# Scatters ahead of a turn's layernorm steps, angle table by chunk with clearing on another engine, last roots by ScalarE

## The chip, the cores and the metric

The kernel runs on one core of a Trainium2 chip. Times are device microseconds (us) of that core; the time of a version is the median of its runs. The engines named below are TensorE (PE; its weight loads are shown as PEld), VectorE (DVE), ScalarE (ACT), GpSimd (POOL) and SyncE (SP). SP only issues DMAs here. Each engine works through its own instructions in the order in which they were put on its queue, and waits on semaphores for what the others produce.

## The reference

Sixteen sequences of 512 tokens with 128 channels pass through a linear attention block and a mixture of experts, each followed by a layernorm over the sum with its input. What matters, shortened:

```python
q, k, v = silu(x @ Wq), silu(x @ Wk), x @ Wv      # 16 heads of 8
lrpe(t) = concat(t * cos(theta * pos), t * sin(theta * pos))
energy = einsum('bhnd,bhmd->bhnm', lrpe(q), lrpe(k)) * tril
out = layernorm((energy @ v) @ Wo * sigmoid(x @ G1 @ G2)) * gamma + beta
x = layernorm(x + out)
probs = softmax(rmsnorm(x) @ router.T)            # 8 experts, 2 a token, capacity 1280
routed = scatter_add(expert(x[dispatch]) * weight)
shared = (silu(x @ sg) * (x @ su)) @ sd
x = layernorm(x + shared + routed)
```

## The kernel before

The tokens are cut into 64 tiles of 128, four to a sequence. The work has four stages.

**Opening.** Constants are made: masks, cleared buffers and the table `cst_tok` of cosines and sines, four chunks of 128 positions, which every sequence shares. `theta` is loaded with one DMA that writes the same row to all 128 partitions (L201). VectorE multiplies it by the positions (L318, L319), brings the angles into range (L320 to L325; chunk 0 first, then chunks 1 to 3 in one go), and ScalarE takes the sines (L330). GpSimd meanwhile writes the masks and clears, one after the other, four pairs of value buffers (`vpad`, `vlow`, L291 and L294), `zero` (L301) and `empty` (L303). The product G1 G2 is put into the weight tile `W` by VectorE (L335); the first projection waits for it.

**Attention turns.** A loop over turns t from -2 to 64 works on three tiles at a time, and its program order is the order on every engine. A turn projects tile t+2 (`project`: pq on PE; six ScalarE instructions; `hat` by VectorE L386), transposes tile t+1 (`turn_over`: pt on PE; kT, q, qT by ScalarE), makes the energies of tile t (`energies`: 32 small matmuls L444, masked to `et` by VectorE L451), and the values of tile t-1 (`values`: up to 56 small matmuls L468, L477, L486; `oT` by ScalarE L492), and then the state of tile t+1 (`remember`, L422, L433). Between them, `advance(turns)` gives the generator `after(b)` of a finished sequence one step (output projection, two layernorms, transposing for the router): its roots are taken by GpSimd with a power of -0.5 (L109), as is `rms` (L542). `sprinkle` gives the router one or more steps, and `shared(t)` puts in a step of the shared expert. At the end of a turn, `scatter_behind` issues two scatters: each is an indirect DMA by GpSimd (L671) that writes 128 rows of x1 to their experts' slots in DRAM. The first is put behind a one-column product `beat` (L688) that waits for `oT` of tile t-1. The DRAM buffers are cleared by 16 DMAs of SyncE, one in each of turns 0 to 15 (`fill`), eight from `zero`, eight from `empty`.

**Experts.** Eight experts, 1280 rows each; the results are scattered back by GpSimd.

**End.** The rest of the shared expert's steps runs on PE; beside it, `add_up` adds the experts' rows and `finish_lot` normalises a lot of tiles: statistics on VectorE (L101, L103), variance plus epsilon (L107), the root by GpSimd (L109), minus mean times root (`nb`, L910), then one ScalarE instruction for each tile (`res`, L913), and a DMA out. The last sequence is four lots of one tile. Each call of `an_end` advances one lot by one step; once the shared steps are used up, lots follow one another.

The turn of the loop, at its end (lines of the profile):

```python
            if 0 <= t + 1 < NT:
                remember(t + 1)
            advance(turns, "narrow")
            advance(turns)
            sprinkle(t, 4)
            if left:

                scatter_behind(oTs[(t - 1) // NC][:, ds((t - 1) % NC * P, 1)])
                scatter_behind()
```

Of the kernel before, what the change touches and what calls it, by code (L numbers as in the profile page):

```python
# [10 lines left out]
F32 = mybir.dt.float32  # L11
I32 = mybir.dt.int32
AF = mybir.ActivationFunctionType
ALU = mybir.AluOpType
# [5 lines left out]
P = 128  # L20
# [15 lines left out]
C1 = 6.28125  # L36
C2 = 2029.0 / 2 ** 20
C3 = 2.0 * math.pi - C1 - C2
# [9 lines left out]
def tile_kernel(  # L48
# [37 lines left out]
    nc.gpsimd.memset(neghalf, -0.5)  # L86
    x1 = keep.tile([P, NT, R], F32, name="x1")
# [23 lines left out]


    def shared_steps(b):
# [6 lines left out]
        def gate_half(i):  # L120
            if i % half == 0:
                h[i // half] = hp.tile([P, half, N], F32, tag="h", name=f"h_{b}_{i}")
            pool, tag = home["g"]
            pg = pool.tile([P, N], F32, tag=tag, name=f"pg_{b}_{i}")
            nc.tensor.matmul(pg, sg_sb[:, ts(i, P)], seq, start=True, stop=True)  # L125
            sl = sp.tile([P, N], F32, tag="sl", name=f"sl_{b}_{i}")
            nc.scalar.activation(sl, pg, AF.Silu)  # L127
            h["s", i] = sl

# [30 lines left out]
    done = set()  # L160
    latest = [None]
# [15 lines left out]
    with ExitStack() as ph:  # L177
# [21 lines left out]
        with tc.manual_schedule(engines=ORDERED):  # L199
            th_sb = cst.tile([P, D + HALF], F32, name="th_sb")  # L200
            nc.sync.dma_start(th_sb, theta.partition_broadcast(P))  # L201
# [15 lines left out]
            nc.gpsimd.memset(rw_sb, 0.0)  # L217
# [3 lines left out]
            load_x(1)  # L221
# [3 lines left out]
            nc.sync.dma_start(bet, beta.partition_broadcast(P))  # L225

# [19 lines left out]
            expi = cst.tile([P, E], I32, name="expi")  # L246
            nc.gpsimd.iota(expi, pattern=[[1, E]], base=0, channel_multiplier=0)
            expf = cst.tile([P, E], F32, name="expf")
            nc.vector.tensor_copy(expf, expi)
            first = cst.tile([P, E], F32, name="first")  # L250
            nc.vector.tensor_scalar(first, expf, -1.0, float(E), ALU.mult, ALU.add)
            startrow = cst.tile([P, E], F32, name="startrow")
            nc.vector.tensor_scalar(startrow, expf, float(CAP), float(-NSLOT), ALU.mult, ALU.add)
            count = cst.tile([P, E], F32, name="count")
            nc.vector.memset(count, 0.0)
            goes_on = {}
            for n in sorted({(b1 - b0) * NC for b0, b1 in groups}):
                goes_on[n] = cst.tile([P, E, n + 1], F32, name=f"goes_on{n}")
                nc.gpsimd.memset(goes_on[n], 1.0)
                nc.gpsimd.memset(goes_on[n][:, :, 0], 0.0)  # L260


            ones = cst.tile([P, P], F32, name="ones")
            nc.vector.memset(ones, 1.0)

            causal = cst.tile([P, 3, HALF], F32, name="causal")
            nc.gpsimd.memset(causal, 1.0)
            for block, at in ((0, 0), (0, HALF), (1, HALF), (2, 0)):
                rows = causal[at : at + HALF, block, :]
                nc.gpsimd.affine_select(  # L270
                    rows, rows, pattern=[[1, HALF]], compare_op=ALU.is_ge, fill=0.0, base=0, channel_multiplier=-1
                )
            tri = cst.tile([P, P], F32, name="tri")
            nc.gpsimd.affine_select(
                tri, ones, pattern=[[1, P]], compare_op=ALU.is_gt, fill=0.0, base=0, channel_multiplier=-1
            )
# [7 lines left out]
            )  # L284


            NVP = 4
            vpads = []
            for i in range(NVP):
                vp = cst.tile([P, 4, 4, 40], F32, name=f"vpad{i}")  # L290
                nc.gpsimd.memset(vp, 0.0)  # L291

                vl = cst.tile([P, 8, 40], F32, name=f"vlow{i}")
                nc.gpsimd.memset(vl, 0.0)  # L294
                vpads.append((vp, vl))
# [4 lines left out]
            zero = hp.tile([P, 4 * N], F32, tag="h", name="zero")  # L300
            nc.gpsimd.memset(zero, 0.0)  # L301
            empty = hp.tile([P, NS, R], F32, tag="h", name="empty")
            nc.gpsimd.memset(empty, 0.0)  # L303
            nc.gpsimd.memset(empty[:, :, D], NOBODY)


            pg = ps_w.tile([P, D], F32, tag="w", name="pg12")
            nc.tensor.matmul(pg, g1t_sb, g2_sb, start=True, stop=True)

            cst_tok = cst.tile([P, NC, 2, 16, 2, 8], F32, name="cst_tok")
            scratch = hp.tile([P, 2, NC, D + HALF], F32, tag="h", name="scratch")
            ang, turns_ = scratch[:, 0], scratch[:, 1]
            for c0, c1 in ((0, 1), (1, NC)):
                a, k = ang[:, c0:c1, :], turns_[:, c0:c1, :]
                for c in range(c0, c1):
                    nc.vector.tensor_scalar(ang[:, c, 0:D], th_sb[:, 0:D], pos[:, 0, c : c + 1], None, ALU.mult)  # L318
                    nc.vector.tensor_scalar(ang[:, c, D:], th_sb[:, D:], pos[:, 1, c : c + 1], None, ALU.mult)  # L319
                nc.vector.tensor_scalar(k, a, 1.0 / (2.0 * math.pi), MAGIC, ALU.mult, ALU.add)  # L320
                nc.vector.tensor_scalar(k, k, MAGIC, None, ALU.subtract)
# [5 lines left out]
                for c in range(c0, c1):  # L327
                    for s, (from_, scale, bias) in enumerate([(turns_, -1.0, half_pi), (ang, 1.0, 0.0)]):
                        for to, n0, n1 in ((cst_tok[:, c, 0], 0, D), (cst_tok[:, c, 1, 1::2], D, D + HALF)):
                            nc.scalar.activation(  # L330
                                to[:, :, s, :], from_[:, c, n0:n1].rearrange("p (h d) -> p h d", d=8), AF.Sin,
                                scale=scale, bias=bias,
                            )
                if c0 == 0:
                    nc.vector.tensor_copy(  # L335
                        W[:, 0:384].rearrange("p (h n) -> p h n", n=24)[:, :, 8:16], pg.rearrange("p (h d) -> p h d", d=8)
                    )
            for c0, c1 in ((0, 1), (1, NC)):
                nc.vector.tensor_copy(
                    cst_tok[:, c0:c1, 1, 0::2].rearrange("p c h s d -> p c h (s d)"),  # L340
                    cst_tok[:, c0:c1, 0, 0::2].rearrange("p c h s d -> p c h (s d)"),
                )
            nc.vector.tensor_scalar(wo_sb, wo_sb, 0.5, None, ALU.mult)
            nc.vector.tensor_copy(x1[:, :, D], toki)
# [14 lines left out]
        def project(t):  # L359
# [376 lines left out]
        with tc.manual_schedule(engines=ORDERED):  # L736
            for t in range(-2, NT + 1):
                coming, here, left = 0 <= t + 2 < NT, 0 <= t < NT, 0 <= t - 1 < NT
                stopped("wait")
                if coming:  # L740
                    if (t + 2) % NC == 0 and 2 <= (t + 2) // NC + 1 < B:
                        load_xT((t + 2) // NC + 1)
                        load_x((t + 2) // NC + 1)
                    project(t + 2)
                if t == 2:
# [54 lines left out]
    with ExitStack() as ph:  # L800
# [96 lines left out]
        def finish_lot(lot):  # L897
# [8 lines left out]
            rs = rstd_of(mv[:, :, 1], n, LN_EPS)  # L906
            yield True
            yield True
# [120 lines left out]
```

## Time and profile before

| what | value |
|---|---|
| time, median of 3 runs (lowest, highest) | 888.75 us (888.18, 888.76) |
| the profiled execution's own time | 912.27 us |
| its span, from the first to the last instruction | 910.6 us |
| mean granted TensorE clock | 0.981 |
| busy share of the span: PE, DVE, ACT, POOL | 93%, 61%, 49%, 38% |
| DMA share, 0 to 25, 25 to 50, 50 to 75 us | 0.88, 1.00, 0.22 |
| first matmul that works on tokens (pq, L363) | 14.22 us |
| last matmul ends | 888.81 us |
| last `res` of ScalarE starts | 901.64 us |

The views used are the page (busy time, the span in slices, the chain of work that ended last, groups of instructions), the chain and the timeline for chosen stretches, and the waits. In the chain each line is a start, a duration and what was waited for or done; "issue" is time in which an engine waited for nothing that the profile shows. In the timeline a line is start, duration, engine, line of the kernel, operation, output <- inputs, with the idle time before it in brackets and what ended it.

The profiled execution took 23.5 us longer than the median of the plain runs, so places in it and sums over it are its own.

### The profile page before, as it was taken

The page shows a single profiled execution, that of the slowest core. Times are in us where ns is not written, and L with a number is a line of the kernel's source. Part 1 is how long each engine was busy: PE and PEld are TensorE (multiplying, and loading weights), DVE is VectorE, ACT ScalarE, POOL GpSimd, SP SyncE. Part 2 cuts the span into 40 slices and gives each one's busy share as a digit, 9 for nine tenths or more (in the row PEclk, how much of TensorE's full clock was granted, in tenths as well). Part 3 has the DMA queues.
Part 4 walks back from the last instruction along what each step waited for, and adds up shares of the span by engine and source line. Part 5 has one row for each costly group of instructions (what it writes and reads, how often), then busy time and mean ns, then how long its engine had stood idle before and what let it go on. Part 6 is the DMA issues. An engine that isn't in the chain of part 4 may idle for free.

```text
span 910.6 us, 24496 instructions
## 1 busy us (share of the span) xinstructions
PE 843.0 (93%) x9790; PEld 576.5 (63%) x9790; DVE 557.1 (61%) x1687; ACT 442.3 (49%) x1285; POOL 344.2 (38%) x455
## 2 busy tenths in 40 slices
PE   2898999999998999989999999999999999999990
PEld 1676667666755776674566657776677766666670
DVE  6588788987688788878743333333333325884542
ACT  3677677566576757745522223333333332334332
POOL 4023222155655645566666703333333331010011
PEclk9999999999999999999999999999999999999996
DMA  8941111011111111000000053222231004641001
GB/s 288 417 146 33 31 32 32 24 34 55 44 50 50 55 32 39 26 22 22 12 8 2 2 159 94 77 68 60 84 91 62 27 24 125 177 135 34 25 24 46
DMA packets 64338, 62.97 MB, mean 69 GB/s; under 512 B 6179, under 2 KB 55130, under 8 KB 63200
## 3 DMA queue, kind: packets, MB, share of 16 engines
q1 hardware_dynamic: 57392, 50.44, 17.5%
q0 software_dynamic: 6656, 10.69, 3.7%
q8 instruction: 77, 1.26, 0.6%
q14 instruction: 37, 0.30, 0.1%
q10 hardware_dynamic: 176, 0.27, 0.1%
HBM read 32.71 MB, written 31.88 MB: 71 GB/s over the span
## 4 chain that ended last, share of the span: by engine, by line
PE 78%; DVE 14%; issue 3%; ACT 3%; DMA 1%; POOL 0%; POOLq 0%; DVEq 0%; ACTq 0%
PE pd L143 11%; PE pg L125 11%; PE pu L133 11%; PE ped L856 8%; PE peg L940 8%; PE peu L942 8%; PE pe L444 4%; PE pq L363 4%; DVE et L451 4%; PE pout L486 3%; PE pt L399 2%; PE pout L477 2%; PE pout L468 1%; PE po L501 1%; DVE st L101 1%
## 5 line engine op out<-in xcount | busy, mean ns | idle before, releaser
L109 POOL TENSOR_TENSOR rstd<-ve,neghalf 128x4 f32<-128x4 f32 (+1 forms) x51 | 52.4, 1028 | 259.0 <-DVE ve L107 224.0
L671 POOL DMA_INDIRECT xg_dram<-x,idx x128 | 132.2, 1033 | 37.7 <-issue 32.1
L127 ACT ACTIVATE sl<-pg 128x512 f32<-128x512 f32 x128 | 76.0, 596 | 127.6 <-PE pg L125 113.2
L862 POOL DMA_INDIRECT y_dram<-y,to x80 | 77.6, 970 | 154.2 <-ACT y L860 154.2
L945 DVE TENSOR_TENSOR eh<-esl,peu 128x512 f32<-128x512 f32 (+1 forms) x96 | 57.5, 599 | 128.1 <-PE peu L942 123.7
L125 PE MATMUL pg<-x1T,sg_sb 128*128 128x512 f32 x256 | 134.0, 605 | 2.1 <-DVE h L134 0.9
L451 DVE TENSOR_TENSOR et<-pe,causal 128x384 f32<-128x384 f32 x256 | 124.4, 547 | 18.0 <-PE pe L444 17.8
L134 DVE TENSOR_TENSOR h<-sl,pu 128x512 f32<-128x512 f32 x128 | 87.6, 684 | 75.5 <-PE pu L133 57.6
L133 PE MATMUL pu<-x1T,su_sb 128*128 128x512 f32 x256 | 131.4, 595 | 0.4 <-DVE x1T L148 0.4
L143 PEld LDWEIGHTS pd<-sd_sb,h 128*128 128x128 f32 x1024 | 119.6, 193 | 5.5 <-issue 5.5
L143 PE MATMUL pd<-sd_sb,h 128*128 128x128 f32 x1024 | 122.6, 276 | 0.0
L856 PEld LDWEIGHTS ped<-rd,eh 128*128 128x128 f32 x640 | 84.0, 192 | 24.6 <-issue 22.7
L940 PE MATMUL peg<-xgT,rg 128*128 128x512 f32 (+1 forms) x192 | 84.6, 522 | 0.0
L942 PE MATMUL peu<-xgT,ru 128*128 128x512 f32 (+1 forms) x192 | 84.4, 521 | 0.0
L856 PE MATMUL ped<-rd,eh 128*128 128x128 f32 x640 | 84.3, 275 | 0.0
L944 ACT ACTIVATE esl<-peg 128x512 f32<-128x512 f32 (+1 forms) x96 | 50.5, 526 | 56.0 <-PE peg L940 53.9
L133 PEld LDWEIGHTS pu<-x1T,su_sb 128*128 128x128 f32 x256 | 46.1, 192 | 45.8 <-issue 39.3
L860 ACT ACTIVATE y<-ped,wt 128x128 f32<-128x128 f32 x80 | 29.4, 367 | 84.6 <-PE ped L856 79.9
L125 PEld LDWEIGHTS pg<-x1T,sg_sb 128*128 128x128 f32 x256 | 44.8, 193 | 39.0 <-issue 33.9
L363 PE MATMUL pq<-W,xT 128*128 128x384 f32 x128 | 61.5, 564 | 7.8 <-DVE W L335 6.9
L444 PE MATMUL pe<-q,kT 32*64 32x192 f32 x2048 | 61.9, 338 | 0.8 <-issue 0.8
L386 DVE TENSOR_TENSOR hat<-qk,cst_tok 128x512 f32<-128x512 f32 x64 | 45.5, 711 | 23.3 <-ACT qk L371 22.6
(164 smaller groups left out, 1285.6 us busy)
## 6 DMA issues: line engine op xcount, KB each, us to landing
y_dram<-zero SPq DMA_DIRECT2D x8, 1024.0 KB
y<-y_dram SPq DMA_DIRECT2D x32, 256.0 KB, 3.2
xT<-xt SPq DMA_DIRECT2D x16, 384.0 KB, 6.5
xg_dram<-empty SPq DMA_DIRECT2D x8, 660.0 KB, 15.7
xg<-xg_dram SPq DMA_DIRECT2D x8, 660.0 KB
x<-x SPq DMA_DIRECT2D x16, 256.0 KB, 4.6
o<-res SPq DMA_DIRECT2D x15, 256.0 KB, 2.3
xg_dram<-x,idx POOLq DMA_INDIRECT x128
```

Source lines behind the costliest of these rows:

```text
L125: nc.tensor.matmul(pg, sg_sb[:, ts(i, P)], seq, start=True, stop=True)
L133: nc.tensor.matmul(pu, su_sb[:, ts(i, P)], seq, start=True, stop=True)
L134: nc.vector.tensor_tensor(h[i // half][:, i % half, :], h.pop(("s", i)), pu, ALU.mult)
L143: nc.tensor.matmul(pd, h[k][:, i - k * half, ts(c, P)], sd_sb[:, i, :], start=(i == 0), stop=(i == IS // P - 1))
L363: nc.tensor.matmul(pq[:, :, 0:24], xts[b][:, c, 0:P], W[:, 0:384].rearrange("p (h n) -> p h n", n=24), start=True, stop=True)
L444: nc.tensor.matmul(pes[g][mine, s], kT[rows, s, mine], q2[rows, s, 3 * i : 3 * i + 3], start=(s == 0), stop=(s == 1),)
L451: nc.vector.tensor_tensor(et.rearrange("p s k n -> p s (k n)"), pes[g].rearrange("p s k n -> p s (k n)"), causal.rearrange("p k n -> p (k ...
L671: i = nc.gpsimd.indirect_dma_start(out=xg_dram[:, :], out_offset=bass.IndirectOffsetOnAxis(ap=idx[:, k, t : t + 1], axis=0), in_=x1[:, t, ...
L856: nc.tensor.matmul(pd, h[:, i, ts(c, P)], got[e][2][:, i, :], start=(i == 0), stop=(i == IR // P - 1))
L862: i = nc.gpsimd.indirect_dma_start(out=y_dram[:, :], out_offset=bass.IndirectOffsetOnAxis(ap=to[:, at : at + 1], axis=0), in_=y, in_offset ...
L940: nc.tensor.matmul(pg[:, :n], rg_sb[:, ts(i, P)], xgTs[e][:, ds(o0, n)], start=True, stop=True)
L942: nc.tensor.matmul(pu[:, :n], ru_sb[:, ts(i, P)], xgTs[e][:, ds(o0, n)], start=True, stop=True)
```

## The change

Four things are edited.

*Opening.* `theta` is loaded as one row to one partition and spread to all by a matmul with ones (`pth`), copied to `th_sb` by ScalarE; the loads of g1t, g2 move from ScalarE's queue to SyncE's, and the first tile's quarter of xT is loaded ahead of the rest. VectorE makes the angles one chunk at a time (`angles`), with a reduction in two parts instead of three; chunks 0 and 1 before the loop, 2 and 3 in turns 0 and 1 (`beginning`), with the sines of 1, 2, 3 in turns -1, 0, 1. GpSimd clears only two of the four pairs of value buffers, and a product with an angle of chunk 0 holds it until those angles are done; the other two pairs, `zero` and `empty` are cleared by ScalarE copies of a zero column (`nought`), the last two at the end of turns 0 and 1. The copy of G1 G2 into `W` goes from VectorE to ScalarE. On ScalarE's queue the sines of chunk 0 stand behind the six instructions of the first projection. Constants of the router are made at the end of turn 2.

*Fills.* The 16 clearing DMAs start one turn later.

*Turn.* The two scatters stand ahead of the turn's second pair of `advance` calls. On GpSimd's queue this moves the second root of each sequence (L109) and `rms` (L542) behind the two scatters of their turn; the first root of a sequence, which is issued in the middle of a turn, stays ahead. No other engine's order changes by it.

*End.* Behind the last Silu, ScalarE loads its table for Sqrt, and lots that take their root after that take it on ScalarE, with a reciprocal on VectorE (`rstd_by_root`), in place of L107 and L109: three lots of four tiles and the four of one. One waiting step less is taken for them.

```diff
+    def rstd_by_root(var, n):
+
+        root = small.tile([P, n], F32, tag="ve", name="root")
+        nc.scalar.activation(root, var, AF.Sqrt, bias=eps_col)
+        r = small.tile([P, n], F32, tag="rstd", name="rstd")
+        nc.vector.reciprocal(r, root)
         return r
...
+            if (b, i) == (B - 1, IS // P - 1):
+
+                warm_root = small.tile([P, 1], F32, tag="warm_root", name="warm_root")
+                nc.scalar.activation(warm_root, eps_col, AF.Sqrt)
+                roots.append(warm_root)
...
-            th_sb = cst.tile([P, D + HALF], F32, name="th_sb")
-            nc.sync.dma_start(th_sb, theta.partition_broadcast(P))
+            th_row = cst.tile([1, D + HALF], F32, name="th_row")
+            nc.sync.dma_start(th_row, theta.unsqueeze(0))
...
-            load_xT(0)
             g1t_sb = cst.tile([8, D], F32, name="g1t_sb")
-            nc.scalar.dma_start(g1t_sb, g1t)
+            nc.sync.dma_start(g1t_sb, g1t)
             g2_sb = cst.tile([8, D], F32, name="g2_sb")
-            nc.scalar.dma_start(g2_sb, g2)
+            nc.sync.dma_start(g2_sb, g2)
+            xts[0] = wk2.tile([P, NC, P + HALF], F32, tag="xT", name="xT_0")
+            nc.sync.dma_start(xts[0][:, 0:1], xt[0, :, 0:1])
+            nc.sync.dma_start(xts[0][:, 1:], xt[0, :, 1:])
+            ones = cst.tile([P, P], F32, name="ones")
+            nc.vector.memset(ones, 1.0)
+            zcol = cst.tile([P, 1], F32, name="zcol")
+            nc.vector.memset(zcol, 0.0)
...
+                if i < 2:
+                    nc.gpsimd.memset(vp, 0.0)
+                    nc.gpsimd.memset(vl, 0.0)
+            def nought(tile_, n):
+                nc.scalar.copy(tile_, zcol.to_broadcast([P, n]))
+            pth = ps_w.tile([P, D + HALF], F32, tag="w", name="pth")
+            nc.tensor.matmul(pth, ones[0:1, :], th_row, start=True, stop=True)
+            th_sb = cst.tile([P, D + HALF], F32, name="th_sb")
+            nc.scalar.copy(th_sb, pth)
+            pg = ps_w.tile([P, D], F32, tag="w", name="pg12")
+            nc.tensor.matmul(pg, g1t_sb, g2_sb, start=True, stop=True)
+            for vp, vl in vpads[2:]:
+                nought(vp.rearrange("p a b d -> p (a b d)"), 640)
+                nought(vl.rearrange("p a d -> p (a d)"), 320)
+            nc.scalar.copy(
+                W[:, 0:384].rearrange("p (h n) -> p h n", n=24)[:, :, 8:16], pg.rearrange("p (h d) -> p h d", d=8)
+            )
...
+            turns_of = cst.tile([P, D + HALF], F32, name="turns_of")
+            nc.vector.tensor_scalar(turns_of, pth, 1.0 / (2.0 * math.pi), None, ALU.mult)
+        def angles(c, th):
+            a, size, k, whole = scratch[:, c], scratch[:, NC + c], scratch[:, 8], scratch[:, 9]
+            both = ((slice(0, D), pos[:, 0, c : c + 1]), (slice(D, D + HALF), pos[:, 1, c : c + 1]))
+            for m, at in both:
+                nc.vector.tensor_scalar(k[:, m], turns_of[:, m], at, MAGIC, ALU.mult, ALU.add)
+            nc.vector.tensor_scalar(whole, k, MAGIC, -C1, ALU.subtract, ALU.mult)
+            for m, at in both:
+                nc.vector.scalar_tensor_tensor(a[:, m], th[:, m], at, whole[:, m], ALU.mult, ALU.add)
+            nc.vector.tensor_scalar(k, k, MAGIC, -C2, ALU.subtract, ALU.mult)
+            nc.vector.tensor_tensor(a, a, k, ALU.add)
+            nc.vector.scalar_tensor_tensor(size, a, -1.0, a, ALU.mult, ALU.max)
+            nc.vector.tensor_scalar(a, a, -PI_BELOW, PI_BELOW, ALU.max, ALU.min)
+        def sines(c):
+            for s, (from_, scale, bias) in enumerate([(scratch[:, NC + c], -1.0, half_pi), (scratch[:, c], 1.0, 0.0)]):
+                for to, n0, n1 in ((cst_tok[:, c, 0], 0, D), (cst_tok[:, c, 1, 1::2], D, D + HALF)):
+                    nc.scalar.activation(
+                        to[:, :, s, :], from_[:, n0:n1].rearrange("p (h d) -> p h d", d=8), AF.Sin,
+                        scale=scale, bias=bias,
+                    )
+        def same(c):
+            nc.vector.tensor_copy(
+                cst_tok[:, c, 1, 0::2].rearrange("p h s d -> p h (s d)"),
+                cst_tok[:, c, 0, 0::2].rearrange("p h s d -> p h (s d)"),
+            )
+        with tc.manual_schedule(engines=ORDERED):
+            angles(0, pth)
+            sines(0)
+            angles(1, th_sb)
+            same(0)
 
+            nc.gpsimd.tensor_tensor(causal[:, 0, 0:1], scratch[:, 0, 0:1], zcol, ALU.mult)
...
+        def constants_of_routing():
+            nc.gpsimd.iota(expi, pattern=[[1, E]], base=0, channel_multiplier=0)
+            nc.vector.tensor_copy(expf, expi)
+            nc.vector.tensor_scalar(first, expf, -1.0, float(E), ALU.mult, ALU.add)
+            nc.vector.tensor_scalar(startrow, expf, float(CAP), float(-NSLOT), ALU.mult, ALU.add)
+            nc.vector.memset(count, 0.0)
+            for g in goes_on.values():
+                nc.gpsimd.memset(g, 1.0)
+                nc.gpsimd.memset(g[:, :, 0], 0.0)
...
+        def beginning(t):
+            if t == -1:
+                sines(1)
+            elif t == 0:
+                angles(2, th_sb)
+                sines(2)
+            elif t == 1:
+                angles(3, th_sb)
+                sines(3)
+        def beginning_done(t):
+            if t == 0:
+                nought(zero, 4 * N)
+            elif t == 1:
+                nought(empty.rearrange("p r d -> p (r d)"), NS * R)
+                nc.gpsimd.memset(empty[:, :, D], NOBODY)
+            elif t == 2:
+                constants_of_routing()
...
-            scratch = hp.tile([P, 2, NC, D + HALF], F32, tag="h", name="scratch")
-            ang, turns_ = scratch[:, 0], scratch[:, 1]
-            for c0, c1 in ((0, 1), (1, NC)):
-                a, k = ang[:, c0:c1, :], turns_[:, c0:c1, :]
-                for c in range(c0, c1):
-                    nc.vector.tensor_scalar(ang[:, c, 0:D], th_sb[:, 0:D], pos[:, 0, c : c + 1], None, ALU.mult)
-                    nc.vector.tensor_scalar(ang[:, c, D:], th_sb[:, D:], pos[:, 1, c : c + 1], None, ALU.mult)
-                nc.vector.tensor_scalar(k, a, 1.0 / (2.0 * math.pi), MAGIC, ALU.mult, ALU.add)
-                nc.vector.tensor_scalar(k, k, MAGIC, None, ALU.subtract)
-                for part in (C1, C2, C3):
-                    nc.vector.scalar_tensor_tensor(a, k, -part, a, ALU.mult, ALU.add)
-                nc.vector.tensor_scalar(a, a, -PI_BELOW, PI_BELOW, ALU.max, ALU.min)
-                nc.vector.scalar_tensor_tensor(k, a, -1.0, a, ALU.mult, ALU.max)
...
+            if 0 < t < NC:
+                same(t)
...
+                beginning(t)
...
-                if 0 <= t < 16:
-                    fill(t)
+                if 1 <= t < 17:
+                    fill(t - 1)
...
                 if 0 <= t + 1 < NT:
                     remember(t + 1)
+                if left:
+
+                    scatter_behind(oTs[(t - 1) // NC][:, ds((t - 1) % NC * P, 1)])
+                    scatter_behind()
                 advance(turns, "narrow")
                 advance(turns)
                 sprinkle(t, 4)
-                if left:
-
-                    scatter_behind(oTs[(t - 1) // NC][:, ds((t - 1) % NC * P, 1)])
-                    scatter_behind()
+                beginning_done(t)
...
-            rs = rstd_of(mv[:, :, 1], n, LN_EPS)
+
+            rs = rstd_by_root(mv[:, :, 1], n) if roots else rstd_of(mv[:, :, 1], n, LN_EPS)
             yield True
-            yield True
+            if not roots:
+                yield True
```

More of the change, by code (lines that the diff above doesn't have):

```diff
@@ L33 @@
 FLT_MIN = 2.0 ** -126
-C1 = 6.28125
-C2 = 2029.0 / 2 ** 20
-C3 = 2.0 * math.pi - C1 - C2
+C1 = 102944.0 / 2 ** 14
+C2 = 2.0 * math.pi - C1
 MAGIC = 1.5 * 2.0 ** 23
@@ L86, in tile_kernel @@
     nc.gpsimd.memset(neghalf, -0.5)
+    eps_col = keep.tile([P, 1], F32, name="eps_col")
+    nc.gpsimd.memset(eps_col, LN_EPS)
     x1 = keep.tile([P, NT, R], F32, name="x1")
@@ L110, in rstd_of @@
         return r
+    def rstd_by_root(var, n):
[3 more added lines that the diff above has]
+        nc.vector.reciprocal(r, root)
+        return r
     def shared_steps(b):
@@ L160, in tile_kernel @@
     done = set()
+    roots = []
     latest = [None]
@@ L216, in tile_kernel @@
             rw_sb = cst.tile([P, 32], F32, name="rw_sb")
-            nc.gpsimd.memset(rw_sb, 0.0)
+            nc.vector.memset(rw_sb, 0.0)
             gam = cst.tile([P, D], F32, name="gam")
@@ L220, in tile_kernel @@
             load_xT(1)
-            load_x(1)
             nc.sync.dma_start(wo_sb, wo)
@@ L225, in tile_kernel @@
             nc.sync.dma_start(bet, beta.partition_broadcast(P))
+            load_x(1)
             posi = cst.tile([P, NC], I32, name="posi")
@@ L243, in tile_kernel @@
             nc.vector.tensor_scalar(par[:, 1:2], bitf, 1.0 / 16, None, ALU.mult)
[L246 to L263, printed above, removed]
@@ L264, in tile_kernel @@
-            nc.vector.memset(ones, 1.0)
+            NVP = 4
+            vpads = []
+            for i in range(NVP):
+                vp = cst.tile([P, 4, 4, 40], F32, name=f"vpad{i}")
+                vl = cst.tile([P, 8, 40], F32, name=f"vlow{i}")
+                vpads.append((vp, vl))
+                if i < 2:
[3 more added lines that the diff above has]
+                nc.scalar.copy(tile_, zcol.to_broadcast([P, n]))
@@ new lines, in tile_kernel @@
+            nc.scalar.copy(
+                W[:, 0:384].rearrange("p (h n) -> p h n", n=24)[:, :, 8:16], pg.rearrange("p (h d) -> p h d", d=8)
+            )
+            cst_tok = cst.tile([P, NC, 2, 16, 2, 8], F32, name="cst_tok")
+            zero = hp.tile([P, 4 * N], F32, tag="h", name="zero")
+            empty = hp.tile([P, NS, R], F32, tag="h", name="empty")
+            scratch = hp.tile([P, 10, D + HALF], F32, tag="h", name="scratch")
+            turns_of = cst.tile([P, D + HALF], F32, name="turns_of")
@@ L266, in tile_kernel @@
+        with tc.manual_schedule(engines=ORDERED):
[3 more added lines that the diff above has]
+            same(0)
             causal = cst.tile([P, 3, HALF], F32, name="causal")
+            nc.gpsimd.tensor_tensor(causal[:, 0, 0:1], scratch[:, 0, 0:1], zcol, ALU.mult)
             nc.gpsimd.memset(causal, 1.0)
[L268 to L276, printed above, removed]
             bmask = cst.tile([P, 64], F32, name="bmask")
@@ L284, in tile_kernel @@
             )
[L287 to L295, printed above, removed]
-            toki = cst.tile([P, NT], I32, name="toki")
-            nc.gpsimd.iota(toki, pattern=[[P, NT]], base=0, channel_multiplier=1)
-            zero = hp.tile([P, 4 * N], F32, tag="h", name="zero")
@@ L301, in tile_kernel @@
[L301 to L312, printed above, removed]
-            scratch = hp.tile([P, 2, NC, D + HALF], F32, tag="h", name="scratch")
-            ang, turns_ = scratch[:, 0], scratch[:, 1]
@@ L315, in tile_kernel @@
-            for c0, c1 in ((0, 1), (1, NC)):
-                a, k = ang[:, c0:c1, :], turns_[:, c0:c1, :]
-                for c in range(c0, c1):
-                    nc.vector.tensor_scalar(ang[:, c, 0:D], th_sb[:, 0:D], pos[:, 0, c : c + 1], None, ALU.mult)
-                    nc.vector.tensor_scalar(ang[:, c, D:], th_sb[:, D:], pos[:, 1, c : c + 1], None, ALU.mult)
-                nc.vector.tensor_scalar(k, a, 1.0 / (2.0 * math.pi), MAGIC, ALU.mult, ALU.add)
-                nc.vector.tensor_scalar(k, k, MAGIC, None, ALU.subtract)
-                for part in (C1, C2, C3):
-                    nc.vector.scalar_tensor_tensor(a, k, -part, a, ALU.mult, ALU.add)
-                nc.vector.tensor_scalar(a, a, -PI_BELOW, PI_BELOW, ALU.max, ALU.min)
-                nc.vector.scalar_tensor_tensor(k, a, -1.0, a, ALU.mult, ALU.max)
[L327 to L343, printed above, removed]
-            nc.vector.tensor_copy(x1[:, :, D], toki)
+            for block, at in ((0, 0), (0, HALF), (1, HALF), (2, 0)):
+                rows = causal[at : at + HALF, block, :]
+                nc.gpsimd.affine_select(
+                    rows, rows, pattern=[[1, HALF]], compare_op=ALU.is_ge, fill=0.0, base=0, channel_multiplier=-1
+                )
@@ new lines, in tile_kernel @@
+            expi = cst.tile([P, E], I32, name="expi")
+            expf = cst.tile([P, E], F32, name="expf")
+            first = cst.tile([P, E], F32, name="first")
+            startrow = cst.tile([P, E], F32, name="startrow")
+            count = cst.tile([P, E], F32, name="count")
+            goes_on = {}
+            for n in sorted({(b1 - b0) * NC for b0, b1 in groups}):
+                goes_on[n] = cst.tile([P, E, n + 1], F32, name=f"goes_on{n}")
+            tri = cst.tile([P, P], F32, name="tri")
@@ new lines, in tile_kernel @@
+            toki = cst.tile([P, NT], I32, name="toki")
+        def constants_of_routing():
[7 more added lines that the diff above has]
+                nc.gpsimd.memset(g[:, :, 0], 0.0)
+            nc.gpsimd.affine_select(
+                tri, ones, pattern=[[1, P]], compare_op=ALU.is_gt, fill=0.0, base=0, channel_multiplier=-1
+            )
+            nc.gpsimd.iota(toki, pattern=[[P, NT]], base=0, channel_multiplier=1)
+            nc.vector.tensor_copy(x1[:, :, D], toki)
@@ L744, in tile_kernel @@
                     project(t + 2)
+                if t == 0:
+                    nc.vector.tensor_scalar(wo_sb, wo_sb, 0.5, None, ALU.mult)
                 if t == 2:
```

## The prediction

> **What bounds the kernel now.** First the page: PE is busy for 93% of the span. The chain of waits then shows where PE is not the bound: the first 25 us, places of "issue" between 188 and 420 us, and the last 22 us. The change touches these three.
>
> The chain in the opening (start, duration, what):
>
> ```profile
> 0.79 5.24 DMA th_sb<-theta
> ...
> 6.06 2.84 DVE scratch L318
> ...
> 8.97 1.89 DVE scratch L320
> ...
> 10.88 1.23 DVE scratch L321
> ...
> 20.13 0.70 DVE hat L386
> ```
>
> Theta's DMA, then one VectorE instruction after another up to `hat` of tile 0. The timeline says why the first are long:
>
> ```profile
> 6.06 2.84 DVE L318 TENSOR_SCALAR scratch<-th_sb,pos 128x128 f32<-128x128 f32 x1 [2.82 <-DMA th_sb<-theta]
> ...
> 8.89 1.85 POOL L301 MEMSET zero<- 128x2048 f32 x1
> ...
> 10.68 1.31 POOL L303 MEMSET empty<- 128x1320 f32 x1
> ...
> 14.08 0.28 DVE L318 TENSOR_SCALAR scratch<-th_sb,pos 128x128 f32<-128x128 f32 x1
> ```
>
> The same L318 takes 2.84 us beside GpSimd's clearing and 0.28 without; L320 and L321 end just after the two clears. L318 to L321 last from 6.06 to 12.11; at the later rows' pace it would be 0.93 us, so 5.1 us are lost.
>
> A turn of the scatter stretch:
>
> ```profile
> 335.78 1.04 POOL L109 TENSOR_TENSOR rstd<-ve,neghalf 128x4 f32<-128x4 f32 x1 [5.49 <-DVE ve L107]
> ...
> 337.16 1.03 POOL L671 DMA_INDIRECT xg_dram<-x,idx  x1 [0.17 <-issue]
> ...
> 338.44 0.33 PE L486 MATMUL pout<-et,vpad 128*32 128x64 f32 x5 [0.46 <-issue]
> ...
> 338.50 0.98 POOL L671 DMA_INDIRECT xg_dram<-x,idx  x1 [0.30 <-issue]
> ...
> 339.19 0.33 PE L486 MATMUL pout<-et,vpad 128*32 128x64 f32 x5 [0.42 <-issue]
> ...
> 339.95 0.40 PE L486 MATMUL pout<-et,vpad 128*32 128x64 f32 x11 [0.42 <-issue]
> ```
>
> GpSimd waits 5.49 us for the variance, takes the root, and only then issues the scatters, whose `oT` was copied at 332.40. They then run beside PE's small matmuls, which stop three times.
>
> The end, chain of waits, one lot:
>
> ```profile
> 890.76 0.18 DVE ve L107
> ...
> 891.10 1.02 POOL rstd L109
> ...
> 892.14 0.16 DVE nb L910
> ```
>
> **Opening, part by part.** I follow the new order by hand, in us.
> - Theta's row. No row shows one descriptor's landing: between 2.3 (median of `o<-res`) and 5.24 (now). It is first on SyncE's queue, so I take 2.4: 3.2. `pth` by pg12's row (0.76 for 128 columns) 1.1: 4.3; copy 0.3, `turns_of` 0.3: 4.9. `angles` of a chunk: L318/L319 pairs start 0.36 apart, one-input 192 wide 0.27, two-input 0.37, two-input pair about 0.48; sum 2.5. Chunk 0 ends at 7.4, with GpSimd held.
> - ScalarE clears 640+320 twice: by L549 (512 wide, 0.59) 2.1, to 6.7; `W` copy 7.0. pq(0) to its Silu took 2.1 (14.22 to 16.33): 9.1; six instructions 1.07; sines of chunk 0, 0.98: 11.2.
> - GpSimd's masks, 2.1 us, fall on VectorE's chunk 1: 9.9 if they don't hold it, 12.1 if they do; by the L318 row mostly, 11.8. Copy and `hat`(0): 12.7, before 20.83.
> - `hat`(1) 14.0, pst and state 14.7, chunk 2 17.2, its sines 18.1, Silu and `hat`(2) 19.2, first `et` 19.4 (before 26.89). Chunk 3 24.0, sines 24.9, `hat`(3) 26.0, second `et` 26.0 (before 29.57); clearing `zero`, 1.9, hides behind VectorE. Third turn: ScalarE has 0.7 + 1.82 + 0.27 + clearing `empty` 1.28 + Silu 0.35: `et` 30.4 (34.27). Fourth, at ScalarE's 3.2 a turn: 33.6 (37.86).
>
> So 7.5 us of lead shrink to 4.3, since two chunks of angles now lie inside turns. 0.84 of the 4.3 is an "issue" stall of before (33.08), leaving 3.4.
>
> A rule speaks against it: the Trainium skill, "TensorE: Matmul & The Clock Gate", section "Part 1: The HAM clock gate", says that PE runs at half clock until about 3.4 us of sustained work, and falls back after an idle window of about 3.4. The trace is harsher: after only 1.78 us of idleness (38.41) the two pq matmuls took 1.58 for 0.84, and clock 0.56 is granted from 40 to 42 us. The new order idles PE some 2 us before the third turn's transposes. By the rule this costs nothing, by the row one slow turn, 1.8, of which the 1.28 of clearing hides 1.1. I take the row: 0.7 lost. **Opening: -2.7**, between -6 (theta and masks kind) and +1.5 (theta at 6, two slow turns).
>
> The other edits here cost nothing: xT's two DMAs land while ScalarE clears; the router constants (2.1 us of GpSimd in turn 2) are first read by VectorE after that turn's `et`.
>
> **Fills.** They start behind the clear of `zero`, about 22 instead of 11.9. 13.7 MB at the 402 GB/s of 25 to 50 us last 34 us, so full DMAs lie over turns 1 to 9, not up to 4. xT(3) on SyncE's queue stands behind seven fills: lands about 41, wanted about 55. x(4) behind five more is wanted far later. Before, PE lost 3.6 us to "issue" there (33.08, 38.41, 45.81, 51.24); in proportion, 2 more in a profile.
>
> **Turn.** The scatters can start at `oT`, 332.7, and end at 335.4; the variance comes at 335.69. The root and `rms` are now queued behind `beat`, so behind ScalarE's `oT`, 3.0 ahead here. So the root is not delayed; were it 2.7 late, its reader `nb` (L528) comes at 340.88, 4.1 after the root's end: still free. `rms` comes 2.7 later, wanted turns later. Scatters then lie beside wide matmuls. Such a turn loses 1.3 us to stalls, and the chain has seven (from 229 to 393): -9.1 in a profile.
> Are those stalls there in a plain run? The profiled execution took 912.27, the plain median 888.75: 23.5 more. The chain's "issue" pieces over 0.08 us add up to 21.8, nearly all beside scatters or full DMAs, and from 60 to 180 us, with the same matmuls and neither, to 0.7. The stalls thus nearly account for what profiling adds, and I take them as mostly its own. In plain runs, **-0.8** of a possible -9.1, and 0 of the fills' +2.
>
> **End.** For a lot of four, L107, GpSimd's root and hops take 1.38 plus `nb` (890.74 to 892.30). New: hop 0.06, root on ScalarE 0.26 (Exp, 128x64: 0.257), hop 0.04, reciprocal 0.18 (L629 0.20), `nb` 0.18: 0.72, saving 0.84; twice, less 0.08 of waiting, 1.6. But ScalarE's queue now has the roots behind `res`:
>
> ```profile
> 895.56 2.03 ACT L913 ACTIVATE res<-x1T,nb,rstd 128x128 f32<-128x128 f32 x5 [1.57 <-issue]
> ```
>
> Four of these take 1.65, so the first single lot's root starts 1.7 after the last `nb`, where GpSimd's started at 0.8: that lot takes 2.3 instead of 1.52, +0.8. The other three singles take about 1.18 (0.50 until `res` is done, then 0.68) for 1.52: -1.0. **End: -1.8**, between -0.9 and -2.6.
> The table: the Trainium skill, "ScalarE: Activation LUTs", section "What ACT_TABLE_LOAD costs", prices a switch at 2.66 with a drain; the row has 1.28 and the next instruction 0.02 later (254.72, 256.02). Last Silu ends 881.43, first root is wanted at 883.26. By the row it is ready in time, by the rule 1.0 late, still ahead of VectorE's next partial sum at 885.26. Either way 0.
>
> **Sum.** -2.7 - 0.8 - 1.8 = -5.3. From the median: **883.4**. The profile itself: 912.27 - 2.7 - 1.8 - 9.1 + 2 = 900.7, so it should fall by more than the median.
>
> **Rivals.**
> - *The stalls are real* (20%): -2.7 - 1.8 - 9.1 + 2 = -11.6, **877.1**. For it: the stalls lie exactly beside the scatters. Against: the 23.5 us would then need another source.
> - *ScalarE holds the opening and PE stays at half clock* (13%): slower. Place: turns 1 to 8, where ScalarE has sines and clears besides its 3.2 us. A slow turn costs 2.2 (pq, pt, pe 4.2 at 22.65 for 2.4 at 27.22, and the values with it). The opening's 3.4 and the end's 1.8 are used up by 2.4 extra slow turns; with four, 8.8 - 5.2 = +3.6, **892.4**. For it: the 0.56. Against: its gaps of 2 us occur once.
> - *The opening gives nothing* (10%): theta lands at 6 and masks lock VectorE fully; only the end stays, with a little of turns: 888.75 - 1.8 = **887.0**.
> - My forecast: 57%, own range 879.5 to 886.9.
>
> About 0.2% (1.8 us) can be told from no change. Faster: 57 + 20 = 77%; same 10%; slower 13%. Range 874 to 889: it leaves out most of the slower case and the far end of the real stalls.
>
> **What would show it.** In the new profile: L309 to L316 at 0.2 to 0.4 us each; `hat` of tile 0 ending near 12.7; fourth `et` near 33.6; scatters ahead of every second root and no triple stop of PE there; last PE end to last `res` 11.0 instead of 12.8. Wrong if the opening's lead at the tenth turn is under 0.5, or if the plain time falls as much as the profile's.

## The result, and the profile after

The changed kernel takes 877.8 us (876.21 to 879.9), beside 888.71 (888.18 to 888.76) for the kernel before: ratio 0.9885, interval 0.9864 to 0.9905, 10.9 us less. That lies inside the stated range; the forecast, 883.4, had the sign right and half the size. Its profiled execution took 876.59, not 900.7.

The kernel before runs at two levels, 887 to 893 us in the comparison above and the first group of experiments and 905 to 915 in the other two groups, and since the kernels of one group ran on one chip, but the three groups on three different chips, times below are compared within a group only. "Quiet" below names the first level, "stopping" the second. The first profile, 912.27, looks like the second, the median beside it, 888.75, like the first.

The page of the kernel after, its first lines (busy time by engine, and the TensorE clock in 40 slices):

```profile
span 874.7 us, 24501 instructions
...
PE 826.3 (94%) x9792; PEld 567.3 (65%) x9792; DVE 554.1 (63%) x1705; ACT 449.4 (51%) x1302; POOL 334.2 (38%) x443
...
PEclk9899999999999999999999999999999999999997
```

PE is busy for the same share as before; what went is time around its work.

The opening in the timeline (start, duration, engine, line, operation, output <- inputs, idle time before it and what ended it):

```profile
2.16 0.97 PE L282 MATMUL pth<-th_row,ones 1*128 1x192 f32 x2 [2.16 <-DVE pos L255]
...
3.91 0.45 DVE L309 TENSOR_SCALAR scratch<-turns_of,pos 128x128 f32<-128x128 f32 x2
...
6.22 0.26 DVE L316 TENSOR_SCALAR scratch<-scratch 128x192 f32<-128x192 f32 x1
...
8.03 1.38 POOL L355 TENSOR_SCALAR_AFFINE_SELECT causal<-causal 64x64 f32<-64x64 f32 x4
...
8.75 0.26 DVE L316 TENSOR_SCALAR scratch<-scratch 128x192 f32<-128x192 f32 x1
...
10.09 0.69 DVE L448 TENSOR_TENSOR hat<-qk,cst_tok 128x512 f32<-128x512 f32 x1
```

The row of theta is there before PE wants it. The angles of chunk 0 take 2.57 us (3.91 to 6.48), and those of chunk 1, beside GpSimd's masks, 2.62 (6.39 to 9.01): the masks hold nothing. The first `hat` ends at 10.78, before 20.83. The first four `et` start at 16.65, 23.11, 27.30 and 30.32, 10.2, 6.5, 7.0 and 7.5 us earlier than in the first profile.

Then the clearing DMAs. The waits of PE between 28 and 66 us (line, what it waited for, us in total, times, longest):

```profile
PE pout L548 <- issue: 3.1, 1, 3.1
PE pe L506 <- issue: 2.8, 2, 2.2
PE pout L539 <- issue: 1.4, 1, 1.4
PE pt L461 <- ACT qk L431: 1.0, 1, 1.0
```

7.2 us of "issue". The windows of PE over the same time (window, length, PE busy and instructions, granted clock, DMA share, GB/s) show when:

```profile
22.00:38.00 16.00, 11.67 (x279) 0.89 1.01 414
38.00:44.00 6.00, 4.73 (x60) 0.72 0.28 69
44.00:63.00 19.00, 15.78 (x449) 1.00 0.97 375
63.00:83.00 20.00, 18.99 (x541) 1.00 0.17 53
```

Three of the four stops begin in the two stretches where DMA is full (1.01 and 0.97), the fourth, at 63.4, just behind the second.

The end, in the timeline:

```profile
868.20 0.49 ACT L981 ACTIVATE res<-x1T,nb,rstd 128x128 f32<-128x128 f32 x1 [0.47 <-ACT root L116]
...
871.65 0.49 ACT L981 ACTIVATE res<-x1T,nb,rstd 128x128 f32<-128x128 f32 x1 [0.47 <-ACT root L116]
```

The last matmul ends at 860.80, the last `res` starts 10.85 us later, as forecast. But it ends at 872.14 and the span at 874.7, 2.5 us later. In the kernel before it ended at 902.13 and the span at 910.6: 8.4 us in which the timeline shows nothing. The prediction never asked what lies there.

### The profile page after: what moved, and what is told of

It reads as the page before. It is cut to its first block, busy times and chain, and to the rows that moved or that the text cites. A ratio compares the mean times of both kernels' runs of the same rounds, so it can differ in the third digit from the quotient of the medians.

```text
span 874.7 us, 24501 instructions
## 1 busy us (share of the span) xinstructions
PE 826.3 (94%) x9792; PEld 567.3 (65%) x9792; DVE 554.1 (63%) x1705; ACT 449.4 (51%) x1302; POOL 334.2 (38%) x443
## 5 line engine op out<-in xcount | busy, mean ns | idle before, releaser
L134 PE MATMUL pg<-x1T,sg_sb 128*128 128x512 f32 x256 | 131.9, 597 | 1.5 <-ACT sl L136 0.7
L110 POOL TENSOR_TENSOR rstd<-ve,neghalf 128x4 f32<-128x4 f32 x44 | 47.2, 1073 | 194.2 <-DVE ve L108 168.0
L1012 ACT ACTIVATE esl<-peg 128x512 f32<-128x512 f32 (+1 forms) x96 | 50.5, 526 | 55.9 <-PE peg L1008 53.9
```

## The experiments

### First group: the kernel before once more, and each part alone (quiet level)

The kernel before, unchanged:

> The kernel before, unchanged, profiled once more. Theory A (the short stops of TensorE beside scatters belong to one profiled execution only): the new profile takes within 3 us of the median of its runs, about 889, and the groups of three stops of 0.42 us beside scatters are gone. Theory B (profiling this kernel always causes them): the new profile again takes 905 to 915 with a median of 889. Theory C (they are real in every run): profile and runs would be alike and both would hold the stops.

889.72 us (888.07 to 890.78); its profiled execution took 890.38, with a span of 888.7, and has no "issue" stop over 0.25 us between 180 and 430 us. In the first profile there are 28 of them there, 11.8 us together. The same scatters beside the same matmuls, now in the timeline of this run:

```profile
347.45 0.66 PE L486 MATMUL pout<-et,vpad 128*32 128x64 f32 x32
...
347.60 1.03 POOL L671 DMA_INDIRECT xg_dram<-x,idx  x1 [0.17 <-issue]
...
347.90 0.65 PE L422 MATMUL pst<-vpad,hat 128*32 128x64 f32 x16
```

32 matmuls go through unbroken while the scatter runs. So the profile alone adds nothing here; theory A holds for this group. What it left out, that whole groups of runs stop, came later.

Only the scatters moved:

```diff
+                if left:
+                    scatter_behind(oTs[(t - 1) // NC][:, ds((t - 1) % NC * P, 1)])
+                    scatter_behind()
                 advance(turns, "narrow")
                 advance(turns)
                 sprinkle(t, 4)
-                if left:
-                    scatter_behind(oTs[(t - 1) // NC][:, ds((t - 1) % NC * P, 1)])
-                    scatter_behind()
```

> The kernel before with only the scatters moved ahead of the turn's layernorm steps. Theory A (stops not there in plain runs): 0.8 us less at most, 888. Theory B (stops real in plain runs): up to 9 us less, 880. Theory C (what the opening and the end leave of the 10.9 us measured, about 1.5 to 3 us, is this part's): 886 to 887.5.

890.34 us beside 889.18, ratio 1.0011 (1.0003 to 1.0019): all three theories miss, it costs about 1 us. The timeline shows where, first for the kernel before (profiled again), then for this run:

```profile
305.49 0.23 DVE L599 TENSOR_TENSOR prob<-prob,tot 128x64 f32<-128x64 f32 x1
...
306.41 1.30 POOL L502 TENSOR_TENSOR x<-x,bet 128x512 f32<-128x512 f32 x1
```

```profile
303.88 1.15 POOL L542 TENSOR_TENSOR rms<-sq,neghalf 128x4 f32<-128x4 f32 x1
...
304.52 1.83 DVE L599 TENSOR_TENSOR prob<-prob,tot 128x64 f32<-128x64 f32 x1
...
305.02 1.25 POOL L502 TENSOR_TENSOR x<-x,bet 128x512 f32<-128x512 f32 x1
...
306.28 0.28 DVE L148 TENSOR_TENSOR x1T<-pd,x 128x128 f32<-128x128 f32 x1
...
306.61 0.43 PE L422 MATMUL pst<-vpad,hat 128*32 128x64 f32 x16 [1.38 <-DVE x1T L148]
```

With the scatters ahead, `rms` comes later on GpSimd, and the sum of x and beta (L502), which waited behind the two scatters, now follows `rms` at once: it starts 1.4 us earlier, onto VectorE's product L599. That ends with GpSimd's sum and takes 1.83 us, here and again at 353.97, where the kernel before has 0.23; `x1T` and PE wait behind it. The kernel before has one such product too, of 2.04 us at 253.89, where this run has 0.29. The Trainium skill, "SBUF — State Buffer", section "SBUF: two separate sides", says that a VectorE instruction with two inputs in SBUF and a GpSimd operation that reads SBUF exclude each other for the whole instruction, and that the first to start has its way. The row agrees that one waits for the other's end; it does not show that order, since by the rows L599 starts 0.50 us before the sum and is the one held.

Only the roots of the last lots on ScalarE (`rstd_by_root` and its table load, as in the change):

> The kernel before with only the roots of the last lots moved to ScalarE. In the profile after, the last matmul's end to the last res is 10.85 us instead of 12.85: 2.0 us less, 886.7, if the end adds to the rest without overlap. Rival: ScalarE's longer queue delays a gate matmul of the last sequence and eats it: 888 to 889.

881.81 us beside 889.18, ratio 0.9912 (0.9890 to 0.9933): 7.4 us less, four times what was forecast for it. At turn 63 this run leads the kernel before by 0.14 us, so all of it is at the end. The last `res` ends 2.1 us earlier; the span ends 8.0 earlier. The rest of 5.9 is the stretch behind the last `res`. The timeline leaves out drains and semaphores; the trace has their records. Those of GpSimd, and the last `res`, in us from the start of the span:

```
kernel before (profiled again)
878.90 8.99  GpSimd  DRAIN
878.93 0.54  GpSimd  TENSOR_TENSOR rstd        ends 879.47
879.75 0.49  Scalar  ACTIVATE res              ends 880.25
882.06       Sync    last of its own           waits for the others
887.94       GpSimd  EVENT_SEMAPHORE           the drain has ended at 887.89
888.67       end of the span

kernel after
846.63 9.46  GpSimd  DRAIN                     ends 856.09
846.66 1.01  GpSimd  TENSOR_TENSOR rstd        ends 847.67
871.65 0.49  Scalar  ACTIVATE res              ends 872.14
873.90       Sync    last of its own
873.93       GpSimd  EVENT_SEMAPHORE
874.67       end of the span
```

At the end of the program all engines meet, and GpSimd comes to the meeting only when its drain has ended, 8.42 us after its last operation in both kernels. Before, that last operation was the root of the last lot, so 8.42 us stood open. After, GpSimd has been free since 847.67.

Only the opening:

> The kernel after with the scatters back behind the layernorm steps and the last roots back on GpSimd: the opening alone. Theory A (the opening's lead of 5.9 us at turn 12 lasts to the end): 883. Theory B (the lead is 7.5 us, as at turn 17, because one slow-clock stretch goes too): 881. Forecast of record for this part: 2.7 us, 886.

885.0 us beside 889.18, ratio 0.9950 (0.9932 to 0.9968): 4.2 us less. The profile's lead over the kernel before of this group is 10.0 us at the first `hat`, 5.5 at turn 12 and 5.4 at turn 63. The lead stays, as theory A has it, but the time lies 1.0 from the 886 of record and 2.0 from theory A's 883; the 2.7 on record was 1.5 too small. The parts sum to 7.4 + 4.2 - 1.2 = 10.4, for 10.9 measured together.

### Second group: the drain, the sum, the clearing, the held product (stopping level, kernel before 910.65)

One GpSimd product behind the last `nb`:

```diff
             nc.vector.scalar_tensor_tensor(nb, mv[:, :, 0], -1.0, rs, ALU.mult, ALU.mult)
+            if lot[1] == NT:
+                last = small.tile([P, 1], F32, tag="last", name="last")
+                nc.gpsimd.tensor_tensor(last, nb, neghalf[:, 0:1], ALU.mult)
```

> The kernel after, with one product of one column by GpSimd added behind the last nb, whose result nobody reads. Theory D (at the program's end all engines wait for a drain of GpSimd, whose record in the trace ends 8.4 us after GpSimd's last operation: 899.10 against 890.68 in the kernel before): the product ends near 871.9 of the profile, the drain near 880.3 and the span near 880.9, for 874.7: 6.1 to 6.2 us more, a median of 884. Theory E (the end's gain came from the shorter chain of roots, and GpSimd's last operation has no cost of its own): no change, 877.8.

```profile
877.77 0.19 POOL L981 TENSOR_TENSOR last<-nb,neghalf 128x1 f32<-128x1 f32 x1 [23.99 <-DVE nb L978]
877.77 0.49 ACT L984 ACTIVATE res<-x1T,nb,rstd 128x128 f32<-128x128 f32 x1 [0.48 <-ACT root L116]
```

The product is beside the last `res` and delays nothing. Yet the span ends at 887.2, 8.9 us behind the end of that `res`, and the drain's record ends 8.42 after the product. Theory D holds: 0.19 us of work costs 6.4 us of end. Every profile of this study agrees. From the end of the last `res` to the end of the span:

| GpSimd's last operation is | profiles | us |
|---|---|---|
| a root or the product in the last lot | before (twice), scatters alone (twice), opening alone, sum later, this one | 8.4 to 8.9 |
| some 24 us earlier | after (twice), end alone, opening and end, three with spread clears | 2.5 to 2.6 |

The time itself, 889.13 us, ratio 0.9769 (0.9740 to 0.9798), does not tell it from the kernel after in the third group (0.9750), whose kernel before is 3.8 lower; the reading rests on the rows.

The opening and the end together (the kernel after with the scatters put back):

> The kernel after with only the scatters back behind the layernorm steps: the opening and the end together. If the parts add up (7.4 for the end alone, 4.2 for the opening alone, scatters 1.2 in the loss): 877.6, and up to 1.4 below the kernel after, 876.5, because the slow-clock stretch near 358 and the stop of 1.4 at turn 52 go. Rival (the scatter move gains once the opening is short): 878.5 to 880.

898.82 us, ratio 0.9874 (0.9847 to 0.9901): 11.8 us less than the kernel before, as the sum of the two parts alone, 11.6. The absolute forecasts missed, since the group runs at the stopping level: this profile again has "issue" stops over 0.25 us in the stretch of the scatters, 29 of them and 12.1 us together, as the first profile had.

Clearing spread over the turns, at most one DMA in a turn, issued by ScalarE (shortened; `zero` has 256 columns in place of 2048):

```diff
-                nc.sync.dma_start(y_rows[:, i, :], zero)
+                nc.scalar.dma_start(y_rows[:, i, :].rearrange("p (a n) -> p a n", n=N // 2), zero...)
...
-                if 1 <= t < 17:
-                    fill(t - 1)
...
+                if 3 <= t < 11:
+                    fill(t + 5)
+                elif 11 <= t < 27 and t % 2:
+                    fill((t - 11) // 2)
```

> As no_scatter, and the 16 clearing DMAs are issued by ScalarE one in a turn (turns 3 to 10, then every second turn to 25) from a block of zeros of 256 columns, so that DMA is never full for long. Theory F (TensorE's issue stops at 30.8, 36.2, 56.0 and 63.4 of the profile after, 7.2 us together, are its instruction pages of 16 KB waiting behind the clearing DMAs): these stops go, 5 to 8 us less than no_scatter, 870 to 872. Theory G (the stops have another cause, or the turns then wait for ScalarE): the same as no_scatter, 877.

892.36 us beside 898.82 for the kernel without this edit: 6.5 us less, within the 5 to 8 forecast. No "issue" stop over 0.25 us is left below 100 us. The windows of this run, as above:

```profile
22.00:38.00 16.00, 13.08 (x325) 0.89 0.13 50
38.00:44.00 6.00, 6.00 (x168) 1.00 0.78 278
44.00:63.00 19.00, 17.52 (x452) 1.00 0.51 180
63.00:83.00 20.00, 18.53 (x410) 0.92 0.52 169
```

The edit also shortens ScalarE's clear of `zero` from 1.90 to 0.41 us. That is not where the gain lies: up to turn 3 this run is 1.4 to 1.7 us behind the one without the edit, and from turn 3 to turn 5, where the first two stops were, it gains 6.5. (At turn 63 these two profiles are 3.6 us apart; the one without the edit took 2.3 less than the median of its runs.) The new queue and the new order of the DMAs were not tried apart from the spreading.

The trace's DMA records show that PE's instructions come by DMA too, in pages of 16 KB: 77 pages for its 2 x 9792 instructions, 64 bytes for each. Beside each of the stops at 30.8, 36.2, 56.0 and 63.4 of the kernel after there is one page (its record starts at 29.8, 37.0, 55.9 and 61.6), and PE goes on 1.3 to 1.4 us after that record's end. So it is for every stop over 0.25 us below 100 us, 36 in the eleven profiles that have any: each ends 1.2 to 1.6 us after the end of a page's record. During the four stops of the kernel after the DMAs of data take 81 to 103% of the 16 DMA engines' time. So the stops are waits for pages, and the edit that took the crowd away took them away; how the queues share the engines is not shown. The Trainium skill, "Runtime: NRT & Kernel Launch", section "Instruction fetch mechanics", calls the cost of crossing such a page mostly hidden; with DMA near full, PE stood for 7.2 us beside four of them.

GpSimd's sum of x and beta one step later, with the scatters moved:

```diff
-            nc.gpsimd.tensor_tensor(x_sb, x_sb, bet.unsqueeze(1).to_broadcast([P, NC, D]), ALU.add)
             yield
+            nc.gpsimd.tensor_tensor(x_sb, x_sb, bet.unsqueeze(1).to_broadcast([P, NC, D]), ALU.add)
```

> The kernel before with the scatters moved ahead, as in scatter_only, and GpSimd's sum of x and beta moved one step later. Theory H (in scatter_only VectorE's product L599 takes 1.83 us in place of 0.23 at turns 52 and 60, held while GpSimd sums x and beta, and x1T and TensorE wait behind it): L599 is back at 0.23 there, the stop of 1.38 at 305 is gone, 1.0 to 1.5 us less than scatter_only, 889. Rival (the later roots and rms themselves cost it): 890.3, as scatter_only.

897.12 us, ratio 0.9846 (0.9817 to 0.9875). The mechanism shows: L599, by its line, took at most 1832 ns of seven in scatter_only and takes at most 294 here.

```profile
L599 DVE TENSOR_TENSOR prob<-prob,tot x7: 191/292/1832, 159.8 to 431.3; 128x64 f32<-128x64 f32 x3, 128x128 f32<-128x128 f32 x2, 128x32 f32<-128x32 f32 x2
```

```profile
L599 DVE TENSOR_TENSOR prob<-prob,tot x7: 191/225/294, 156.9 to 435.9; 128x64 f32<-128x64 f32 x3, 128x128 f32<-128x128 f32 x2, 128x32 f32<-128x32 f32 x2
```

(Minimum, median, maximum in ns; the first is scatter_only, the second this run.) At 305.99 of this run L599 lies beside `rms` alone and takes 0.23, so it is the sum that held it. What that is worth can't be read from this time, since scatter_only ran at the other level.

### Third group: what each is worth at the stopping level (kernel before 906.89)

> The kernel after, unchanged, beside the three below. The chips differ: on one the kernel before took 889, with no short stops of TensorE beside scatters; on the other 910, with them. Theory I (the scatter move pays only where these stops are): where the kernel before takes 889, this takes 878; where it takes 910, this takes 883 (the run with GpSimd's extra product, 889.1, less 6.1).

883.34 us, ratio 0.9750 (0.9725 to 0.9775): 23.5 us less, more than twice the gain at the quiet level.

> The kernel before with only the scatters moved, once more. Theory I: where the kernel before takes 910, 12 to 15 us less, about 897; where it takes 889, 1 us more, 890. Rival (the scatter move is worth nothing anywhere, and the gain of the last runs has another source): 910 there.

893.54 us, ratio 0.9851 (0.9827 to 0.9875): the scatter move alone takes off 13.4 us here. Theory I holds. In a turn of the kernel after at this level the scatters run beside wide matmuls:

```profile
324.13 1.03 POOL L733 DMA_INDIRECT xg_dram<-x,idx  x1 [0.20 <-issue]
325.24 1.16 PE L563 MATMUL po<-wo_sb,oT 128*128 128x128 f32 x8 [0.70 <-ACT qk L431]
325.46 1.01 POOL L733 DMA_INDIRECT xg_dram<-x,idx  x1 [0.30 <-issue]
...
327.16 0.43 PE L539 MATMUL pout<-et,vlow 128*32 128x64 f32 x16
327.41 0.63 PE L548 MATMUL pout<-et,vpad 128*32 128x64 f32 x32
```

They end before the groups of 16 and 32 small matmuls begin, and these go through whole; 5 stops, 1.8 us, are left of 28. The 28 of the first profile each end 0.7 or 1.3 to 1.5 us after a scatter's start, but 0.1 to 8.1 us after a page of instructions, so they are not the waits for pages of the opening. And they cost more than the idle time in brackets: in the first profile five matmuls and a stop take 0.75 us (338.44 to 339.19), where the quiet level has 32 in 0.66, so 0.10 for five. By this estimate a stop costs 0.65 us, and the 28 cost 18. PE's waits from 185 to 420 us, first in the first profile of the kernel before, then here:

```profile
PE pout L486 <- issue: 5.6, 13, 0.5
PE pst L422 <- issue: 3.4, 9, 0.4
PE pout L477 <- issue: 3.1, 8, 0.5
```

```profile
PE po L563 <- ACT qk L431: 4.9, 4, 1.9
PE pout L539 <- issue: 2.0, 8, 0.4
PE pst L484 <- DVE x1T L162: 1.3, 1, 1.3
```

> The kernel after with the clearing DMAs issued by ScalarE one in a turn, as in paced. If this is worth the same beside the moved scatters: 6.5 us less than after_again, 871 where the kernel before takes 889, 876.5 where it takes 910.

877.2 us beside 883.34: 6.1 us less, as beside the unmoved scatters. Against the kernel before 0.9660 (0.9636 to 0.9685): the best version found, faster than both kernels.

> As paced_after, and GpSimd's sum of x and beta one step later, as in bet_later. If the held product L599 costs 1 to 1.5 us in the kernel after too: that much less than paced_after. If not: the same.

877.41 us: no gain. L599 is short again, at most 292 ns, but the time doesn't follow. The held product is real, and what it costs next to the other changes is below what these runs can tell.

## Why the prediction was right or wrong, point by point

**Opening.** Direction and mechanism were right, the size low: 4.2 us measured for 2.7. The terms: theta and the first projection, `hat` ends at 10.78 for 12.7 forecast; masks on chunk 1, taken as mostly holding VectorE, hold nothing (2.62 us for 2.57); `W` is copied at 5.35 for 6.7. The lead that shrinks was forecast as 7.5 to 4.3 and is 10.2 to 7.5 over the first four `et` (the fourth at 30.32 for 33.6). Behind them the fills take most of what is lost: PE's "issue" stops there are 7.2 us, against 4.6 in the kernel before profiled again, and 5.5 is left at turn 12 of the opening alone. So the step "0 of the fills' +2" failed: these stops are in plain runs, and the edit that spreads the clears gets 6 us out of them. The slow turn forecast at half clock came, from 22.6 us, in 2.6 us of idleness, and stretched this matmul (1.65 us for 0.91 later):

```profile
23.15 1.65 PE L423 MATMUL pq<-W,xT 128*128 128x384 f32 x2 [2.61 <-ACT vlow L444]
```

But the rival of many slow turns did not: in the first 100 us the kernel after has three stretches of 3.4 us at half clock, and the kernel before three as well.

**Scatters.** The step that failed is the sentence that the stops "nearly account for what profiling adds". In the thirteen profiled executions made since, each lay within 2.8 us of the median of its own runs, so profiling adds nothing of that size. The 23.5 us lay between two levels at which whole groups run. Adding up the "issue" pieces (21.8) was right and taking them for the profile's own was wrong; one profile beside runs of another group can't tell these apart. The -0.8 thus holds nowhere: +1.2 at one level, -13.4 at the other. The rival "the stalls are real" describes the second, but its -9.1 is too small: it takes 1.3 us a turn from the idle time of three stops, and at 0.65 us a stop the same seven turns give 13.7. The test written down for it, that the plain time falls as much as the profile's, could not be read in the comparison on record, where the profile before was of the other level. There the move gave nothing, so the total near that rival's 877.1 is a coincidence.

**End.** The chain's terms were right: first single lot 2.31 between two `nb` for 2.3, the next 1.15 for 1.18, last matmul to last `res` 10.85 for 11.0. The table for Sqrt was loaded at 853.45 in 1.28 us and the next instruction began 0.01 later, so the 1.28 of the row and not the 2.66 that the prediction weighed against it was the price, and it was hidden. What failed is the sum's end: -1.8 took the last `res` for the end of the program. 8.4 us lay behind it in the profile of before, and they belonged to the engine that the change sets free. Measured 7.4 = 2.0 of chain, and 5.4 of the uncovered drain (5.9 in the profile).

**The sum.** -5.3 forecast, -10.9 measured: +1.5 more from the opening, 5.6 more from the end, and 2.0 less from the scatters make 10.4; 0.5 is within the intervals of the parts.

## What to carry to other kernels

Subtract the last visible instruction's end from the span before pricing the end of a kernel: if several us are left, ask which engine's drain they are, and end that engine's work that much earlier (here 8.4 us), however short it is. Spread bulk DMAs that nobody waits for over the stages that have DMA to spare, since an engine with many small instructions gets its code by DMA too. And when one profile and the plain runs differ by some per cent, profile the kernel again beside its own runs before calling the difference the profiler's.

## What the runs showed of the hardware that was not expected

- GpSimd's drain at the end of a program ends 8.42 us after its last operation, whether that is a root of 128x4 (1.01 us), of 128x1 (0.54), or a product of one column (0.19).
- The same kernel takes 889 us in one group of runs and 907 to 911 in two others, with the granted clock alike (0.983 in the profile of the one, 0.981 in the first profile, which has the stops). These two profiles of the kernel before are within 0.2 us of each other from turn 10 to turn 30 and 21.2 us apart at turn 63, and what stands out is stops of some 0.42 us of PE among small matmuls beside GpSimd's scatters, by the estimate above 18 us. Each of the three groups ran on a chip of its own, so the chip may be the cause; no chip was used for two groups, and nothing was tried on it. Why small matmuls stop there stays open.
- Beside four instruction pages of PE, fetched while DMA was near full, PE stood for 7.2 us, each time until 1.3 to 1.4 us after the page's record ended.
